# A first graph product in seven quarter products, with its column factors prepared a layer sooner

## The chip, the cores and the metric

One core of a Trainium2 chip runs the whole program. The metric is the device time of one execution in microseconds (us). Before the change it is 2473.33 us, the median of three runs (2473.07 to 2473.34).

## What is computed

Sixteen graphs (batches) with 1024 nodes, 128 features a node, and a 1024 x 1024 matrix adj each, all in float32. Two blocks follow each other. The first is one graph layer, the second four graph layers, and each block ends in a residual sum and a layer norm:

```python
# first block
degree = adj.sum(-1)[:, :, None]
s  = einsum('bid,bij->bjd', x, adj) / degree
x1 = layernorm(x + relu(concat([x, s]) @ W.T + b))
# second block: layers i = 0..3
src_agg = einsum('bjv,bij->biv', f @ ws + bs, adj / l2norm_of_rows)
dst_agg = einsum('bjv,bji->biv', f @ wd + bd, adj / l2norm_of_columns)
f = tanh(concat([src_agg, f @ wn + bn, dst_agg]) @ wu + bu)
# f of layers 2 and 3 is joined with inputs of earlier layers
out = layernorm(x1 + f)
```

A batch so needs adj itself, its transpose, the norms of its rows and columns, and one more sum per row (the degree).

## The kernel before

A batch is a sequence on TensorE of: messages and aggregation of layers 0, 1 and 2 of batch b, the first block of batch n = b + 1 (`first_gnn`), and messages and aggregation of layer 3 of batch b. The work that prepares batch n (its matrix, its sums, its factors, its transpose, its norm) is put between the matmuls of batch b. Four engines have a hand-written order: TensorE (PE), VectorE (DVE), ScalarE (ACT) and GpSimd (POOL) execute what the Python code issues, in that order; only SyncE (SP), which issues the DMAs, is ordered by the framework's scheduler. Where one instruction uses what another engine produced, a semaphore wait is added, and what is queued behind it on its engine waits too.

`aggregate` (L565) computes one layer as products of quarters: adj and the messages are cut into halves both ways, and seven products of sums of quarters take the place of eight (the scheme known as Strassen-Winograd). A product is four matmuls of a 128 x 64 stationary operand against 512 columns. Two such matmuls, one for the upper and one for the lower 64 rows of the output, go to TensorE as a pair; one pair is a step. Layers 0 and 1 have 30 steps, layer 2 has 32, layer 3 has 34: first two or more for the nodes' own features, then the products M1 to M4, Z11, Z12 and Z21, each with a DST half (adj, sums T) and a SRC half (adj transposed, sums Q). `events` read finished sums at fixed steps, and `hooks` is a table of step numbers at which other work is issued: a hook at 11 is issued ahead of step 11, on whatever engine its instructions belong to. `between` does the same for the four groups of `messages` (L504), which produce the tiles t and, on VectorE, their sums S1 to S4 (L529 to L532).

The parts that matter here:

- `first_gnn` (L424): x times adj in whole, 8 row blocks x 2 halves of columns = 16 pairs, each half scaled by dinv (the inverse of degree times norm), then four pairs with the weights.
- `sums` (L237): of a row block of the next matrix, the degree (on ScalarE for blocks 0 to 3, L249, on VectorE for 4 to 7, L251), the squares (ScalarE, L252), and their running sum acc on GpSimd (L254, L256). The tile sq has two places, so a square waits for the add that used its place before. For b over 0, blocks 0 to 7 are issued at steps 1, 2, 4, 6, 12, 15, 18 and 20 of layer 1.
- `column_sums` (L259) transposes and reduces acc on VectorE, in the messages of layer 2 (`between` 1); `inverses` (L288, a small matmul pc, then VectorE, then a power on GpSimd) at step 4 of layer 2; `inverse_rows` and `factor_row` (L319, L331) send the factors to DRAM and back, spread over all partitions as cinv; at step 10 `row_inverses` (L304), at step 18 the small matmul rp (`gather_inverses`, L312); at steps 12, 15, 19 and 25 `scale_columns` (L338) multiplies the next matrix by cinv, four row blocks by one half of columns at a time.
- The second norm of batch b - 1 runs in layer 1: y and its sum s (VectorE, L349, L354, L356) at step 0, the small matmul pm at step 11 (`norm_centre`, L359), pv and a power at step 17 (`norm_rstd`, L375); its end and its store are issued in layer 2 at step 4.
- `load(n)` (L190), the next matrix, is issued at step 5 of layer 0. It goes where the matrix of batch b - 1 was; that place serves in layer 3 as a staging place for the rows of adj that are to be transposed, the last of them rows[0], which is transposed at step 0 of the following layer 0 (`rows3`).

Of the kernel before, what the change touches and what calls it, by code (L numbers as in the profile page):

```python
# [8 lines left out]
F32 = mybir.dt.float32  # L9
AF = mybir.ActivationFunctionType  # L10
# [4 lines left out]
P = 128  # L15
# [8 lines left out]
def adj_resnorm_kernel(ctx: ExitStack, tc: tile.TileContext, x, adj, w0, b0, layers, out):  # L24
# [54 lines left out]
    def half(h):  # L79
        return slice(h * HW, (h + 1) * HW)  # L80
# [99 lines left out]
    def by_halves(out, x, y, start=True, stop=True):  # L180

        for s in (slice(V, P), slice(V)):
            nc.tensor.matmul(out[s], x[:, s], y, start=start, stop=stop)  # L183

    def product(name, i=None):
        if i is None:
            return ps_t.tile([P, HW], F32, tag="pt", name=name)
        return ps_p.tile([P, HW], F32, tag=f"p{i}", name=name)
# [47 lines left out]

    def sums(b, a, state, rows):  # L237

        if not state:
            state["cols"] = two.tile([P, 3 * NB], F32, tag="cols", name=f"cols{b}")  # L240
            state["acc"] = one.tile([P, N], F32, tag="row", name=f"acc{b}")
            state["inv"] = two.tile([P, C], F32, tag="inv", name=f"inv{b}")
            nc.gpsimd.memset(state["inv"][:, 3 * NB:], 0.0)
        cols, acc = state["cols"], state["acc"]
        for i in rows:
            sq = two.tile([P, N], F32, tag="sq", name=f"sq{b}_{i}")
            degree = cols[:, 2 * NB + i:2 * NB + i + 1]
            if i < BPH:
                nc.scalar.activation(sq, a[:, i, :], AF.Copy, accum_out=degree)  # L249
            else:  # L250
                nc.vector.reduce_sum(degree, a[:, i, :], axis=AX.X)  # L251
            nc.scalar.activation(sq, a[:, i, :], AF.Square, accum_out=cols[:, i:i + 1])  # L252
            if i == 1:
                nc.gpsimd.tensor_add(acc, state["sq"], sq)  # L254
            elif i > 1:
                nc.gpsimd.tensor_add(acc, acc, sq)  # L256
            state["sq"] = sq

# [164 lines left out]

    def first_gnn(b, xn, xT, a, dinv):  # L424

        agT = one.tile([P, N], F32, tag="acc", name=f"agT{b}")
        yT = one.tile([P, N], F32, tag="x", name=f"yT{b}")
        for h in (1, 0):
            s = half(h)
            pa = product(f"pa0_{b}_{h}")  # L430
            for i in range(NB):
                by_halves(pa, xn[:, i], a[:, i, s], i == 0, i == NB - 1)
            nc.vector.tensor_mul(agT[:, s], pa, dinv[:, s])
            if h == 1:
                combine_1(quarters(a))
        for h in (1, 0):
            first_weights(b, h, xT, agT, yT)
        return yT

    def first_weights(b, h, xT, agT, yT):  # L440
        s = half(h)
        pw = product(f"pw0_{b}_{h}")
        by_halves(pw, w0T[:, 0], xT[:, s], True, False)
        by_halves(pw, w0T[:, 1], agT[:, s], False, True)
        nc.scalar.activation(yT[:, s], pw, AF.Relu, bias=b0c)

# [33 lines left out]
    def quarters(a):  # L480
        return {(j, h): a[:, j * NJ:(j + 1) * NJ, half(h)] for j in range(2) for h in range(NH)}
# [8 lines left out]
    def combine_1(y):  # L490

        nc.vector.tensor_sub(y[0, 1], y[0, 1], y[0, 0])
# [72 lines left out]
    def aggregate(b, l, feats, msgs, a, at, T, Q, fT, etag, hooks={}, pieces=1):  # L565
# [81 lines left out]
        else:  # L647
# [3 lines left out]
            if l < NL - 1:  # L651
# [5 lines left out]
                (A, True, prod("M3", SRC)),  # L657
                (Z0, False, prod("Z21", SRC) + prod("Z21", DST)),
            ]
# [12 lines left out]

        def steps(groups, rows):
            flat = []
            for m, (acc, first, mms) in enumerate(groups):
                later = [g[1] for g in groups[m + 1:] if g[0] is acc]
                last = not later or later[0]
                for i, (x, y) in enumerate(mms):
                    flat.append((acc[rows], x, y, first and i == 0, last and i == len(mms) - 1))
            return flat  # L680

        up, lo = steps(upper, high), steps(lower, low)
        assert len(up) == len(lo)
# [230 lines left out]
    for b in range(B):  # L914
# [8 lines left out]
        if b == 0:  # L923
            def first_half0():
                nonlocal rinv
                to_x1(0)
                rinv = gather_inverses(0, row_inverses(0, inv))
                column_sums(0, st0)
                for q in (2, 3):
                    scale_rows(rows[q], q, rinv)  # L930

            t = messages(b, 0, feats, wm, {0: first_half0}, with_sums=False)
            cinv = {}
# [35 lines left out]
            def folded(l, part):  # L969
                return lambda *_: part(l, fetched[l])  # L970

            hooks = {2: lambda *_: inverses(0, st0, NB), 3: rows0, 5: folded(2, fold_begin), 7: cinv0,
                     8: folded(2, fold_end), 9: lambda *_: fold_and_scale(3, 0), 11: second0, 12: folded(3, fold_end),
# [5 lines left out]
            xs2 = load_spread(n)  # L979
        else:  # L980
            t = messages(b, 0, feats, wm)
            wm = message_weights(b, 1)
            w = {}
            Q = combined(b, "Q")
# [4 lines left out]

            def next_rows(w=w):  # L990
                combine_1(yt)
                if nxt:
                    w["a"] = load(n)

            hooks = {0: rows3, 3: lambda: combine(4, y, T), 5: next_rows, 7: lambda: combine(2, yt, Q),
                     9: lambda: combine(3, yt, Q), 11: lambda: combine(4, yt, Q)}
            aggregate(b, 0, feats, t, a, at, T, Q, f1, "row", hooks)
# [7 lines left out]

        def sums_of(i):
            return lambda: sums(n, a2, st, (i,))

        hooks = {}
        if b == 0:  # L1010
            def quarters2():
                for i in (2, 3, 4):
                    combine(i, yt, Q)

            hooks = {0: quarters2, 12: lambda: combine(4, y, T)}
            hooks |= {5 + 2 * i if i < 3 else 4 + 3 * i: sums_of(i) for i in ALL}
        else:
            nm = f"1_{b - 1}"
            w = {"ys": summed(f"y{nm}", "xa")}
            sums_of_next = dict(zip((1, 2, 4, 6, 12, 15, 18, 20), map(sums_of, ALL))) if nxt else {}  # L1020

            def begin1(w=w, nm=nm):
                norm_spread(w["ys"], f4, KS)
                w["s"] = norm_sum(w["ys"], KS, nm, back)

            def centre1(w=w, nm=nm):
                w["sq"] = norm_centre(w["ys"], w["s"], KS, nm)
                if nxt:
                    w["xs"] = load_spread(n)

            def squares1(w=w, nm=nm):
                w["v"] = norm_squares(w["sq"], KS, nm)

            def rstd1(w=w, nm=nm):
                w["r"] = norm_rstd(w["v"], KS, nm)

            hooks = {0: begin1, 11: centre1, 14: squares1, 17: rstd1, **sums_of_next}
        aggregate(b, 1, feats, t, a, at, T, Q, f23, "acc", hooks)
        second_norm = w if b else None
        if b:  # L1040
            xs2 = w.get("xs")

# [3 lines left out]

        def end1(w=second_norm):
            if b:
                norm_end(w["ys"], w["r"], KS)
                store(b - 1, w["ys"], KS)  # L1050

        def inverses3():
            inverses(n, st)
            end1()

# [19 lines left out]

        hooks, between = {4: end1}, {}
        if nxt:
            between = {1: sums3}
            hooks = {4: inverses3, 5: factors, 10: factors_of_rows, 11: start3, 12: lambda: scale(0, 1),
                     15: lambda: scale(NJ, 1), 18: factors_gathered, 19: lambda: scale(0, 0), 25: lambda: scale(NJ, 0)}  # L1080
        t = messages(b, 2, feats, wm, between)
        wm = message_weights(b, 3)
        aggregate(b, 2, feats, t, a, at, T, Q, f23, "acc", hooks)
        if nxt:
            dinv = factor_row(n, st, 2, "dinv")
            yT = first_gnn(n, w["xn"], w["xT"], a2, dinv)
            rinv = w["rinv"]
# [5 lines left out]
        if nxt:  # L1093
# [23 lines left out]

            def rstd0(w=w):
                w["r"] = norm_rstd(w["v"], KS, nm)


# [15 lines left out]

            def quarters0(w=w):
                w["T"] = combined(n, "T")
                for i in (2, 3):  # L1140
                    combine(i, y2, w["T"])
                scale_rows(rows[2], 2, rinv)

            def rows1(w=w):
                at2[1] = transposed(n, 1)
                transpose_rows(rows[2], 2, at2)
                scale_rows(rows[3], 3, rinv)
                w["back"] = take_back(b, kept)
                rows[0] = load_rows(n, 0, [place(0)])

# [23 lines left out]
        if nxt:  # L1174
            wm = message_weights(n, 0)
        aggregate(b, 3, feats, t, a, at, T, Q, f4, "row", hooks, 1 if nxt else 2)
        if nxt:
# [57 lines left out]
```

## Time and profile before

| | |
|---|---|
| median of three runs | 2473.33 us (2473.07 to 2473.34) |
| the profiled execution | 2473.83 us |
| its span (first to last instruction) | 2472.0 us |
| granted TensorE clock, mean | 0.998 |
| matmul time of one first product (16 pairs) | 13.73 us |
| GpSimd's add of 128x1024, mean (L256) | 2446 ns |
| SyncE: the next matrix, 8 DMAs of 512 KB | 12.2 us each to landing (median) |

The profile is of one execution. In its rows a start is in us from the span's start, then come the time taken, the engine, the line of the program, the operation, output<-input with shapes, and in brackets the idle time before it with the engine that ended it; "x2" rows merge neighbours. Rows of the chain have start, time, engine, output and line. PE is TensorE, DVE VectorE, ACT ScalarE, POOL GpSimd. A matmul of float32 shows as two records, so a pair is four.

### The profile page before, as it was taken

What the parts mean: (1) busy time and instruction counts of PE and PEld (TensorE: products, weight loads), DVE (VectorE), ACT (ScalarE), POOL (GpSimd) and SP (SyncE); (2) the same over time, 40 slices, a digit from 0 to 9 for tenths busy, and PEclk for the clock granted to TensorE, in tenths of its full rate; (3) what the DMA queues carried; (4) which work ended last, traced back from release to release, by engine and by line L of the source; (5) the groups of instructions that cost most, each with busy time, mean ns of one, the idle gap of its engine ahead of it and who ended that gap; (6) DMA issues with size and microseconds to landing.
All of it is one profiled execution on the core that took longest, in us unless ns stands there. A gap on an engine that the chain in (4) does not pass through costs nothing.

```text
span 2472.0 us, 30281 instructions
## 1 busy us (share of the span) xinstructions
PE 2457.1 (99%) x11573; PEld 1037.2 (42%) x11573; DVE 1689.8 (68%) x2075; ACT 843.1 (34%) x1569; POOL 524.8 (21%) x205
## 2 busy tenths in 40 slices
PE   8999999999999999999999999999999999999998
PEld 5443344433444344443434444334443344433444
DVE  5858667586775857668577685776858667586743
ACT  5415234152341513425143341433415234152321
POOL 4401304013040220402104030040311304013000
PEclk9999999999999999999999999999999999999999
DMA  9517245261543516335172442724427244261410
GB/s 206 101 48 150 51 96 104 63 135 43 115 92 74 117 43 135 77 85 101 46 150 59 98 88 60 152 44 102 94 58 143 52 97 103 64 134 44 94 24 9
DMA packets 363793, 219.66 MB, mean 89 GB/s; under 512 B 150848, under 2 KB 334912, under 8 KB 363648
## 3 DMA queue, kind: packets, MB, share of 16 engines
q1 hardware_dynamic: 362880, 215.36, 41.3%
q0 software_dynamic: 768, 2.36, 0.4%
q8 instruction: 92, 1.51, 0.3%
q14 instruction: 53, 0.43, 0.1%
HBM read 199.17 MB, written 18.46 MB: 88 GB/s over the span
## 4 chain that ended last, share of the span: by engine, by line
PE 97%; DMA 1%; SPq 1%; DVE 0%; ACT 0%; issue 0%; POOLq 0%; DVEq 0%
PE m L692 44%; PE z L692 26%; PE pt L514 16%; PE pa L183 8%; PE pw L183 2%; DMA raw<-in_L_gnn_ws_dram 1%; SPq L458 0%; PE z L562 0%; PE pm L183 0%; DMA a<-in_adj_dram 0%; PE d L562 0%; DMA raw<-in_L_gnn_bs_dram 0%; DMA rows<-in_adj_dram 0%; DMA raw<-in_L_gnn_wn_dram 0%; SPq L131 0%
## 5 line engine op out<-in xcount | busy, mean ns | idle before, releaser
L692 PE MATMUL m<-Q,S 128*64 128x512 f32 x1008 | 446.4, 593 | 0.0
L692 PE MATMUL m<-T,S 128*64 128x512 f32 x1008 | 396.4, 593 | 0.0
L692 PE MATMUL m<-at,t 128*64 128x512 f32 x1008 | 393.5, 593 | 0.0
L692 PE MATMUL m<-a,t 128*64 128x512 f32 x1008 | 390.6, 593 | 0.0
L382 POOL TENSOR_TENSOR rs<-ve,mhalf 128x32 f32<-128x32 f32 x30 | 169.4, 5645 | 871.5 <-DVE ve L380 871.5
L517 DVE TENSOR_TENSOR t<-pt,wm 128x512 f32<-128x512 f32 x256 | 175.4, 690 | 188.6 <-PE pt L514 188.0
L692 PEld LDWEIGHTS m<-Q,S 128*64 128x64 f32 x1008 | 135.7, 137 | 270.8 <-issue 260.9
L256 POOL TENSOR_TENSOR acc<-acc,sq 128x1024 f32<-128x1024 f32 x90 | 220.1, 2446 | 82.2 <-ACT sq L252 79.8
L692 PE MATMUL z<-at,S 128*64 128x512 f32 x504 | 230.1, 594 | 0.0
L692 PE MATMUL z<-T,t 128*64 128x512 f32 x504 | 226.8, 592 | 0.0
L692 PE MATMUL z<-a,t 128*64 128x512 f32 x504 | 226.8, 592 | 0.0
L692 PE MATMUL z<-at,t 128*64 128x512 f32 x504 | 226.6, 592 | 0.0
L692 PE MATMUL z<-a,S 128*64 128x512 f32 x504 | 226.6, 592 | 0.0
L692 PE MATMUL z<-Q,t 128*64 128x512 f32 x504 | 226.6, 592 | 0.0
L596 ACT COPY e<-m 64x512 f32<-64x512 f32 x63 | 36.7, 582 | 528.0 <-PE m L692 527.7
L514 PE MATMUL pt<-wm,f1T 128*128 128x256 f32 x768 | 213.6, 383 | 0.1
L183 PE MATMUL pa<-a,xn 128*64 128x512 f32 x960 | 208.5, 592 | 0.0
L340 DVE TENSOR_TENSOR a<-a,cinv 128x512 f32<-128x512 f32 x250 | 156.7, 694 | 75.5 <-DMA cinv<-dr 73.0
L254 POOL TENSOR_TENSOR acc<-sq,sq 128x1024 f32<-128x1024 f32 x15 | 41.6, 2770 | 761.7 <-ACT sq L252 761.7
L692 PEld LDWEIGHTS m<-at,t 128*64 128x64 f32 x1008 | 120.2, 137 | 143.9 <-issue 143.9
L692 PEld LDWEIGHTS m<-T,S 128*64 128x64 f32 x1008 | 118.9, 137 | 135.4 <-issue 135.4
L692 PEld LDWEIGHTS m<-a,t 128*64 128x64 f32 x1008 | 119.0, 137 | 126.1 <-issue 117.3
(196 smaller groups left out, 3960.9 us busy)
## 6 DMA issues: line engine op xcount, KB each, us to landing
a<-in_adj_dram SPq DMA_DIRECT2D x120, 512.0 KB, 12.2
a<-in_adj_dram SPq DMA_DIRECT2D x360, 128.0 KB, 3.9
rows<-in_adj_dram SPq DMA_DIRECT2D x240, 64.0 KB, 2.9
wm<-wsave SPq DMA_DIRECT2D x16, 512.0 KB, 3.9
xn<-in_x_dram SPq DMA_DIRECT2D x124, 64.0 KB, 2.1
wm<-wsave SPq DMA_DIRECT2D x31, 256.0 KB, 2.7
xs<-in_x_dram SPq DMA_DIRECT2D x60, 128.0 KB, 3.6
cinv<-dr SPq DMA_DIRECT2D x30, 256.0 KB, 5.2
```

Of the source, the lines that this page charges most:

```text
L183: nc.tensor.matmul(out[s], x[:, s], y, start=start, stop=stop)
L254: nc.gpsimd.tensor_add(acc, state["sq"], sq)
L256: nc.gpsimd.tensor_add(acc, acc, sq)
L340: engine.tensor_mul(a[:, i, s], a[:, i, s], cinv[:, s])
L382: nc.gpsimd.tensor_tensor(rstd, ve, mhalf[:, :n], ALU.pow)
L514: nc.tensor.matmul(pt[:, q], f[:, i * P:(i + 1) * P], wm[:, 1 + c], start=(k == 0), stop=(k == nch - 1))
L517: nc.vector.tensor_add(t[j][:, o:o + 2].rearrange("p k a v c -> p k (a v c)"), pt, wm[:, 0][:, None, :].to_broadcast([P, 2, 2 * P]))
L596: nc.scalar.copy(e0[high], A[high])
L692: nc.tensor.matmul(o, x, y, start=start, stop=stop)
```

## The change

For the batches 1 to 15, the first block's product x times adj is computed by the same scheme as the layers: seven products of four matmuls, 14 pairs in place of 16. It needs sums of quarters of x (`first_sums`, in a place of the tag sq) and of adj: T2 in the places of S2, S3, S4 and x, T3 in those of t0 and t1, T4 in that of the layers' T4. As T4 is overwritten, it is computed a second time in layer 3 (`rstd0`). In layers 1 and 2 the product Z21 has its DST half, which reads T4, ahead of its SRC half.

What prepares the next matrix is moved, for b over 0: its load to the beginning of layer 0; the degrees all to ScalarE, four of them at steps 17 and 19 of layer 0 and four in layer 1, as copies in place; the squares of blocks 0 and 1 both at step 1 of layer 1 and the others at 3, 5, 8, 12, 15 and 18; the column sums to step 23 and `inverses` to step 29 of layer 1; `inverse_rows` and `factor_row` to the first group of messages of layer 2; the four scalings to steps 4, 6, 8 and 10 of layer 2, `row_inverses` to 12, `gather_inverses` to 17, x's transpose to 20, and the new sums to 13, 16, 25 and 29. The end of the second norm moves to step 14 of layer 2, its pv behind layer 1. rows[0] gets places of its own (tags xa and acc). For b = 0 the old step numbers stay and the new sums are at 26, 27, 29 and 31. In batch 0 the row factors move behind the third group of messages.

```diff
-            pa = product(f"pa0_{b}_{h}")
-            for i in range(NB):
-                by_halves(pa, xn[:, i], a[:, i, s], i == 0, i == NB - 1)
-            nc.vector.tensor_mul(agT[:, s], pa, dinv[:, s])
-            if h == 1:
-                combine_1(quarters(a))
+        T3 = first_quarter_3(b, y, T2)
+        upper = [(A, True, prod(X[0, 0], y[0, 0])), (Bk, True, prod(S[2], T2)), (A, True, prod(S[3], T3, (0, 1))),
+                 (Z0, True, prod(X[1, 1], T4))]
+        lower = [(Ck, True, prod(S[1], y[0, 1])), (Z1, True, prod(S[4], y[1, 1])), (Dk, True, prod(S[3], T3, (2, 3))),
+                 (Z0, True, prod(X[0, 1], y[1, 0]))]
+        events = {4: m1_and_m4_read, 8: m2_read, 10: m3_read}
...
+    def first_quarter_2(b, y):
+        T2 = [one.tile([P, HW], F32, tag=tag, name=f"f2_{b}_{tag}") for tag in ("S2", "S3", "S4", "x")]
+        for k in range(NJ):
+            nc.vector.tensor_sub(T2[k], y[1, 1][:, k], y[0, 1][:, k])
+        return T2
...
+    def squares_of_row(b, a, state, i):
+        sq = two.tile([P, N], F32, tag="sq", name=f"sq{b}_{i}")
+        nc.scalar.activation(sq, a[:, i, :], AF.Square, accum_out=state["cols"][:, i:i + 1])
+        if i == 1:
             state["acc"] = one.tile([P, N], F32, tag="row", name=f"acc{b}")
+            nc.gpsimd.tensor_add(state["acc"], state["sq"], sq)
+        elif i > 1:
+            nc.gpsimd.tensor_add(state["acc"], state["acc"], sq)
+        state["sq"] = sq
...
-                (Z0, False, prod("Z21", SRC) + prod("Z21", DST)),
+                *((Z0, False, prod("Z21", part)) for part in ((SRC, DST) if l == NL - 1 else (DST, SRC))),
...
-            t = messages(b, 0, feats, wm, {0: first_half0}, with_sums=False)
+            t = messages(b, 0, feats, wm, {0: lambda: to_x1(0), 2: row_factors0}, with_sums=False)
...
+            if nxt:
+                w["a"] = load(n)
+                st = begin_sums(n)
             t = messages(b, 0, feats, wm)
...
+                     9: lambda: combine(3, yt, Q), 11: lambda: combine(4, yt, Q),
+                     17: lambda: degrees(0), 19: lambda: degrees(2)}
...
-            sums_of_next = dict(zip((1, 2, 4, 6, 12, 15, 18, 20), map(sums_of, ALL))) if nxt else {}
+            if nxt:
+                sums_of_next = {1: sums_of(0, 1), 3: sums_of(2), 5: sums_of(3, of=(4,)), 8: sums_of(4, of=(5,)),
+                                12: sums_of(5, of=(6,)), 15: sums_of(6, of=(7,)), 18: sums_of(7),
+                                23: lambda: column_sums(n, st), 29: lambda: inverses(n, st)}
...
-            hooks = {0: begin1, 11: centre1, 14: squares1, 17: rstd1, **sums_of_next}
+            hooks = {0: begin1, 11: centre1, 14: squares1, **sums_of_next}
         aggregate(b, 1, feats, t, a, at, T, Q, f23, "acc", hooks)
         if b:
-            xs2 = w.get("xs")
+            rstd1()
+            second_norm, xs2 = w, w.get("xs")
...
+            scales = [lambda: scale(0, 1), lambda: scale(NJ, 1), lambda: scale(0, 0), lambda: scale(NJ, 0)]
+            if b == 0:
+                between = {1: sums3}
+                hooks = {4: inverses3, 5: factors, 10: factors_of_rows, 11: start3, 18: factors_gathered,
+                         **dict(zip((12, 15, 19, 25), scales))}
+                quarters_at = (26, 27, 29, 31)
+            else:
+                between = {0: factors}
+                hooks = {**dict(zip((4, 6, 8, 10), scales)), 12: factors_of_rows, 14: end1, 17: factors_gathered, 20: start3}
+                quarters_at = (13, 16, 25, 29)
+            hooks |= dict(zip(quarters_at, (quarter1, x_sums, quarter2, quarter4)))
...
-            def rstd0(w=w):
+            def rstd0(w=w, y=y, T=T):
                 w["r"] = norm_rstd(w["v"], KS, nm)
+                combine(4, y, T)
...
+                rows[0] = load_rows(n, 0, [one.tile([P, QB // 2, NH * P], F32, tag=tag, name=f"rows0_{n}_{tag}")
+                                           for tag in ("xa", "acc")])
```

## The prediction

> **What bounds the kernel now.** I read the page first (busy shares, chain, groups), then the chain in order of time for one whole batch (b = 5, from 812.08 us), then the timelines of VectorE, GpSimd and ScalarE in its layer two (l = 1).
>
> ```profile
> PE 2457.1 (99%) x11573; PEld 1037.2 (42%) x11573; DVE 1689.8 (68%) x2075; ACT 843.1 (34%) x1569; POOL 524.8 (21%) x205
> ...
> PE 97%; DMA 1%; SPq 1%; DVE 0%; ACT 0%; issue 0%; POOLq 0%; DVEq 0%
> ...
> L183 PE MATMUL pa<-a,xn 128*64 128x512 f32 x960 | 208.5, 592 | 0.0
> ```
>
> TensorE is the bound, and nothing makes it wait. The third row is the product that the change shortens. The chain gives its price and the places of three small matmuls (start, duration):
>
> ```profile
> 754.79 13.73 PE pa L183 x64
> ...
> 847.15 7.72 PE m L692 x36
> 854.88 0.18 PE pm L183 x4
> ...
> 871.52 7.10 PE pt L514 x32
> 878.62 3.58 PE z L692 x16
> 882.20 0.09 PE pc L183 x4
> ```
>
> Sixteen pairs of 64-column matmuls take 13.73 us, 0.858 a pair; a layer advances by one such step at a time. The batches repeat every 151.68 us (754.79 to 906.47). pm, pc and the like read a VectorE result in the middle of TensorE's queue: late results stop TensorE there. VectorE around pm:
>
> ```profile
> 846.05 0.76 DVE L529 TENSOR_TENSOR S<-t 128x256 f32<-128x256 f32 x2
> 846.85 0.69 DVE L530 TENSOR_TENSOR t<-t,t 128x512 f32<-128x512 f32 x1
> 847.57 0.69 DVE L531 TENSOR_TENSOR S<-t 128x512 f32<-128x512 f32 x1
> 848.30 2.73 DVE L532 TENSOR_TENSOR S<-t,S 128x512 f32<-128x512 f32 x1
> 850.95 1.23 DVE L349 STREAM_TRANSPOSE y<-f23T 128x1024 f32<-128x1024 f32 x1
> 852.22 1.23 DVE L354 TENSOR_TENSOR y<-y,xk 128x1024 f32<-128x1024 f32 x1
> 853.48 1.22 DVE L356 TENSOR_REDUCE s<-y 128x32 f32<-128x1024 f32 x1
> ```
>
> GpSimd at that time, then ScalarE, which feeds it:
>
> ```profile
> 847.71 2.77 POOL L254 TENSOR_TENSOR acc<-sq,sq 128x1024 f32<-128x1024 f32 x1 [53.03 <-ACT sq L252]
> 852.99 5.13 POOL L256 TENSOR_TENSOR acc<-acc,sq 128x1024 f32<-128x1024 f32 x2 [2.51 <-ACT sq L252]
> ```
> ```profile
> 843.04 1.04 ACT L249 ACTIVATE sq<-a 128x1024 f32<-128x1024 f32 x1
> 844.20 1.06 ACT L252 ACTIVATE sq<-a 128x1024 f32<-128x1024 f32 x1
> ```
>
> Two things count. The sum s ends at 854.70 and pm starts at 854.88: no slack. And L532, 0.69 us elsewhere, took 2.73: it began 0.6 us into GpSimd's add, and ended 0.55 after it (850.48).
>
> [...] The trace agrees: 2.73 against 0.69 above, and L621 2.32 at 863.58 inside the add of 862.99 to 865.35; it also shows the turns: GpSimd asked during L531 and went before L532. The reduces (L251, L356) ran at 1.21 beside adds[...]
>
> **The change, part by part.** Measured against the profiled execution: 2473.83 us (span 2472.0 and 1.8 around it), 0.5 over the median.
>
> *Matmuls.* Seven products of four matmuls are 28, 14 pairs for 16: 2 x 0.858 = 1.72 a batch, 15 batches, 25.7 us. The four weight pairs stay. On the path in full: TensorE is the path.
>
> *First product's own operations.* T2, T3 and T4 are 12 subtractions of 128x512 at 0.614 (the rate of L340: 8 in 4.91), 7.4 us; the sums of x are four of half that, some 1.6; eight at 0.69 end it; the two agT multiplies (0.69 each) go. For b over 0, counting on from pc (below): x's transpose must wait until y1 has been stored out of the same place (5.4 us from L387's end to L345 in the trace), after that T2 is complete 1.7 us before TensorE's step 4 of the product asks for it, T3 meets step 8 within 0.1, e1 and e0 are 1.3 and 0.7 ahead of the weight pairs. TensorE's own 14 pairs are the cover: cost 0, at most 0.5 a batch. The T4 recomputed in layer four (2.29) fits into VectorE's 5.54 us wait on GpSimd before L387: 0; uncovered it would be 2.29. DST before SRC in Z21 only frees T4 four steps sooner: 0.
>
> *b = 0.* Its scalings stay at steps 12 to 25 and end at 151.74 in the trace; then combine_1 2.28, two x sums 0.8: 154.9, where TensorE wants them at 148.07: 6.9 us of wait; T3 then misses step 8 by 1.4. Cost 8.4 once (bounds 6 and 9).
>
> *Load of the next matrix, rows0, SP.* The load moves from 824.17 to the end of the transposes at 812.08. In the order of the built program its first DMA stands ahead of eight rows0 DMAs, and the other seven behind them. Rows0: 8 x 0.47 to 0.64 from 812.6, landing 2.9 later: 819.3 to 820.7, scaled by four ScalarE steps of 0.42 by 822.4; the transpose comes up at about 822.5. 0, at most 0.5. The load's first half is in about 15 us after 812 (eight DMAs took some 18 before), ahead of degrees at 829.
>
> *Degrees.* Four ScalarE copies of 1.06 go between m1's and m4's copies of layer one, a gap of 5.67 us: 0. The other four leave VectorE (1.21 each) for ScalarE in layer two. The in-place copy changes nothing.
>
> *Squares, layer two.* Without degrees 0 and 1, the second square ends 2.32 sooner, so GpSimd's first add asks at 845.39 instead of 847.71, and runs to 847.75 (2.36). That is ahead of S3 (L529) at 846.05, which now waits to 847.6; S1 ends at 849.10. Square 2 starts as the first add ends, and the second add asks at 849.07 (1.29 after it); S2 asks at 849.14. 0.07 decides, less than I trust these rows with. (a) Add first: S2 ends 851.98, add three (queued) 854.20, S4 854.75, transpose 855.98, L354 behind add four 858.06, s 859.32, pm 859.50 for 854.88: TensorE 4.6 late. (b) S2 first: add two ends 852.04, S4 852.6, transpose 853.8, L354 behind add three 855.9, s 857.16, pm 857.34: 2.5 late. Lowest, if VectorE wins each further turn: s 855.2, 0.5. S3's own wait (1 us at step 2) is inside these. Queued behind pm is the whole of TensorE.
>
> *Column sums before the end of layer two (steps 23 and 29).* From s: centre 1.6, its square 1.1, degree and square 2.2, m4 copies 1.3, degree and square 2.2, add six 2.6, VectorE's e0 add behind it 0.5, add seven 2.2, e1 add behind that 0.6, transpose and reduce 2.5, handing over 0.3: 17.1 to pc. TensorE needs 0.18 + 18 x 0.858 after pm, and pm is 0.18 after s: 15.8. Wait 1.3, in (a) and (b) alike.
>
> *Scaling sooner.* Before, pc 882.20 to the first scaling 896.54 took 14.34 (sums, power on GpSimd 3.8, two DMAs). Now all 16 multiplies come next: 9.82, then row_inverses 0.15: 24.4 with the hand-over. TensorE gets from pc (step 29) to the rp matmul (step 17 of layer three) in 0.09 + 0.86 + 0.09 + 7.10 + 3.58 + 13 x 0.86 = 22.9. rp waits 1.5; behind it is all of TensorE. Bounds 0.8 to 2, as the DMAs land. Before, rp stood at step 18 with only tiny work ahead of it. The statistics' pv and power at the end of layer two hide behind the messages: 0.
>
> *Start.* rp and pc of batch 0 move later; TensorE waited 1.9 for sp once: gain about 1.
>
> **Sum.** 2473.8 - 25.7 + 8.4 - 1.0 = 2455.5. For the 14 batches b = 1 to 14: (a) 4.6 + 1.3 + 1.5 = 7.4, making 2559; (b) 5.3, making 2530. I take the middle, 6.4, since the turn may fall either way, batch by batch: 2455.5 + 89.6 = 2545. Lowest: 0.5 + 1.3 + 1.5 = 3.3, 2502.
>
> **Rivals.**
> - *The adds don't hold VectorE up this time.* Then s and the column sums are ready in time and only rp waits, 1.5: 2455.5 + 21 = 2476.5, no change. For: S3 has never overlapped an add in the trace. Against: every other two-input operation that did was held.
> - *Faster: all hidden.* Place: the scalings of layer three. If they begin 1.5 us sooner after pc, by a quicker power (2.91 at 126.81) and DMAs, and the adds cost nothing, rp is ready and 2455.5 is left. It decides from 14.34 down to 12.8. Against: VectorE waited for cinv in all 15 batches.
> - *More:* as (a), and rows0 or T3 late by 0.5 each: 2573.
> - That fewer matmuls are not issued is excluded: the built order has 14 pairs.
>
> **Numbers.** 0.2% (about 5 us) is what a measurement tells from no change. Main case with its bounds 2502 to 2562: 0.80, all slower; more than that 0.05; no change 0.07, of which 0.02 over the 5 us; faster 0.08. So slower 0.87, same 0.05, faster 0.08. The range 2495 to 2575 takes in the main case, the worse one and some us of rounding below, and leaves out the other two rivals and tails, about 0.18.
>
> **What would show it.** Period of the first product 154 to 159 us instead of 149.96; VectorE's S3 at over 2 us in layer two, one or two more of S2, S4, L354 stretched; TensorE idle before pm, pc and rp, named as waiting for s, part and sp; 7 us before batch 1's product. If S3 takes 0.4, or TensorE stays at 99%, the main case is wrong; if pm is on time while pc waits, the turns are.

## The result, and the profile after

The changed kernel takes 2548.99 us, the median of four runs (2547.21 to 2552.26), against 2473.23 before (with a fourth run of it): a ratio of 1.0308, 95% interval 1.029 to 1.0326. Its profiled execution took 2547.21 us (span 2545.4), 73.4 more than that of before.

TensorE issues fewer matmuls and is still the busiest engine, but the chain no longer lies on it alone. The page of after, shares of the span and then the chain by engine:

```profile
PE 2469.9 (97%) x11453; PEld 1041.9 (41%) x11453; DVE 1912.2 (75%) x2394; ACT 952.4 (37%) x1786; POOL 540.3 (21%) x205
...
PE 17%; DVE 4%; DMA 2%; issue 1%; SPq 0%; POOL 0%; ACT 0%; DVEq 0%; POOLq 0%; ACTq 0%
```

Before, 11573 matmul records and PE with 97% of the chain; now 120 fewer (15 products by two pairs of four records), and VectorE and DMAs on the chain. (The chain that the page follows back covers a quarter of the span here, so I read from it only which engines appear.) What TensorE waits for is in its own view of waits (us in total, times, longest):

```profile
PE pm L183 <- DVE s L358: 44.9, 14, 3.2
PE m_f L512 <- DVE xn L440: 5.9, 1, 5.9
...
PE m_f L512 <- ACT e_f L489: 2.9, 3, 1.4
PE m L770 <- DVE Q L583: 2.2, 5, 0.8
PE rp L183 <- DVE sp L309: 2.1, 2, 1.2
PE pc L183 <- DVE part L272: 1.8, 3, 0.6
```

pm stops TensorE in each of the 14 batches whose layer two prepares a next matrix, for 3.2 us; batch 1's sums of x once, for 5.9; the other waits are short and rare, rp and pc among them. (Layers one, two and three are from here on, as in the prediction, what the sections ahead of it call layers 0, 1 and 2.) Where pm's delay comes from shows in VectorE's timeline in layer two, the counterpart of the rows of before (S3 is now L616, S1 L617, S2 L618, S4 L619):

```profile
2122.52 2.26 DVE L616 TENSOR_TENSOR S<-t 128x256 f32<-128x256 f32 x2
2124.82 0.69 DVE L617 TENSOR_TENSOR t<-t,t 128x512 f32<-128x512 f32 x1
2125.54 2.79 DVE L618 TENSOR_TENSOR S<-t 128x512 f32<-128x512 f32 x1
2128.36 2.73 DVE L619 TENSOR_TENSOR S<-t,S 128x512 f32<-128x512 f32 x1
2131.02 1.23 DVE L351 STREAM_TRANSPOSE y<-f23T 128x1024 f32<-128x1024 f32 x1
2132.29 2.11 DVE L356 TENSOR_TENSOR y<-y,xk 128x1024 f32<-128x1024 f32 x1
2134.43 1.22 DVE L358 TENSOR_REDUCE s<-y 128x32 f32<-128x1024 f32 x1
```

and in GpSimd's:

```profile
2121.81 2.35 POOL L256 TENSOR_TENSOR acc<-sq,sq 128x1024 f32<-128x1024 f32 x1 [49.67 <-ACT sq L253]
2125.42 7.89 POOL L258 TENSOR_TENSOR acc<-acc,sq 128x1024 f32<-128x1024 f32 x3 [1.26 <-ACT sq L253]
```

Before, S3, S2 and the addition of xk took 0.76, 0.69 and 1.23 and S4 alone was held (2.73). Now S3 (2.26), S2 (2.79), S4 (2.73) and the addition (2.11) are: each waited for the addition on GpSimd that began before it. Taken one by one, the three additions of the last row took 2.36, 2.69 and 2.69: an addition that came up behind another waited in its turn for the operation of VectorE that the other one held. S1 ran free (0.69), in the 1.26 us in which GpSimd waited for the third square. In the kernel before, too, the operations held inside an addition read both operands from SBUF (L532 2.73 for 0.69, L621 2.32 for 0.69). L517, which reads pt from PSUM, took its 0.69 in all 30 cases that begin inside an addition, as at 873.48, with the additions of 871.18 to 875.96. An operation of the first kind is what the prediction calls a two-input one.

Where the time went, by stretches of TensorE's own sequence. Each number is a mean over these 14 batches, worked out from starts in the trace: from the first matmul of the first product to the weights (batches 2 to 14), layer one's products with the messages that follow them, layer two from its first own-feature matmul to pm, from pm to the messages of layer three, and layer three from its first matmul to the next first product:

| us | first product | layer one | to pm | pm to messages | layer three | batch 1's product |
|---|---|---|---|---|---|---|
| before | 13.73 | 29.55 | 9.54 | 16.69 | 27.75 | 13.73 |
| after | 12.33 | 29.80 | 14.02 | 18.27 | 27.78 | 20.36 |

A first product without a wait is 12.02. The sum: 15 x 1.71 less; batch 1's wait 8.3; 13 x 0.31; 14 x 0.25; 14 x 4.48; 14 x 1.58; 14 x 0.03; and 2.0 less at the start. That is -25.7 + 8.3 + 4.0 + 3.5 + 62.7 + 22.1 + 0.4 - 2.0 = 73.3, against 73.4 measured. So 85 of the us lie in layer two.

The 22.1 behind pm look like the late pc that I had forecast, and are mostly not. Columns: window in us, then busy time (and instructions) of PE, PEld, DVE, ACT and POOL, the granted TensorE clock, DMA share and GB/s. The first three windows lie around pm in one batch, the last two in another:

```profile
2132.12:2135.53 3.41, 0.38 (x1) 0.00 (x0) 3.34 (x3) 0.52 (x1) 1.20 (x1) 1.00 0.02 3
2135.53:2138.94 3.41, 3.23 (x12) 1.22 (x14) 1.69 (x3) 1.44 (x2) 0.00 (x0) 0.50 1.08 151
2138.94:2142.36 3.42, 3.42 (x18) 1.12 (x16) 0.87 (x1) 3.38 (x7) 1.64 (x1) 1.00 0.00 0
879.43:882.84 3.41, 1.60 (x6) 0.27 (x2) 3.38 (x3) 1.70 (x3) 2.41 (x1) 1.00 0.00 0
882.84:886.25 3.41, 2.02 (x14) 0.88 (x16) 2.52 (x3) 0.35 (x1) 0.00 (x0) 1.00 0.76 115
```

and TensorE's rows in the first of the two batches:

```profile
2135.71 0.43 PE L183 MATMUL pm<-s,fold 128*64 128x32 f32 x4 [3.20 <-DVE s L358]
...
2136.83 1.06 PE L770 MATMUL m<-T,S 128*64 128x512 f32 x1
...
2137.68 1.06 PE L770 MATMUL m<-T,S 128*64 128x512 f32 x1
...
2139.60 0.59 PE L770 MATMUL m<-T,S 128*64 128x512 f32 x1
```

For 3.41 us TensorE ran at a granted clock of 0.50: matmuls start 0.85 apart in place of 0.43, which costs half of that time, 1.7. In 11 of the 14 batches the trace has such a run of long matmuls behind pm, and there the stretch is 18.3 to 18.5; in the other three (17.6) there is none, and it is there that pc waits for its sum, 0.6.

The falls of the clock behind pm last 3.413 us each, one in batch 1's product (from 148.98) twice that, and they start whole multiples of 3.413 us apart. Cut into windows on this grid from batch 1's product on, the trace has a fall behind every window in which TensorE was recorded idle for 1.99 us or more (3.03 in the first row above), and behind none with 1.95 or less. All 14 waits for pm last 3.2; in the three batches without a fall a border of the grid splits the idle time into 1.81 and 1.39 (the last two rows above), 1.95 and 1.26, 1.67 and 1.54. So in this trace where a wait falls on the grid decides, beside its length.

### The profile page after: what moved, and what is told of

The parts are those of the page before. It is cut to its first block, busy times and chain, and to the rows that moved or that the text cites. A ratio compares the mean times of both kernels' runs of the same rounds, so it can differ in the third digit from the quotient of the medians.

```text
span 2545.4 us, 30905 instructions
## 1 busy us (share of the span) xinstructions
PE 2469.9 (97%) x11453; PEld 1041.9 (41%) x11453; DVE 1912.2 (75%) x2394; ACT 952.4 (37%) x1786; POOL 540.3 (21%) x205
## 3 DMA queue, kind: packets, MB, share of 16 engines
q0 software_dynamic: 768, 2.36, 0.4%
## 5 line engine op out<-in xcount | busy, mean ns | idle before, releaser
L770 PE MATMUL m<-T,S 128*64 128x512 f32 x1008 | 413.8, 612 | 1.6
L770 PE MATMUL m<-at,t 128*64 128x512 f32 x1008 | 413.5, 612 | 0.0
L384 POOL TENSOR_TENSOR rs<-ve,mhalf 128x32 f32<-128x32 f32 x30 | 192.5, 6415 | 973.5 <-DVE ve L382 973.5
L258 POOL TENSOR_TENSOR acc<-acc,sq 128x1024 f32<-128x1024 f32 x90 | 230.5, 2561 | 145.7 <-ACT sq L253 141.7
L256 POOL TENSOR_TENSOR acc<-sq,sq 128x1024 f32<-128x1024 f32 x15 | 35.7, 2379 | 704.4 <-ACT sq L253 704.4
L770 PE MATMUL z<-T,t 128*64 128x512 f32 x384 | 172.9, 592 | 0.0
L601 PEld LDWEIGHTS pt<-wm,f1T 128*128 128x128 f32 x768 | 143.3, 190 | 32.8 <-ACT f1T L783 12.8
```

What stands on the lines that cost most here:

```text
L256: nc.gpsimd.tensor_add(state["acc"], state["sq"], sq)
L258: nc.gpsimd.tensor_add(state["acc"], state["acc"], sq)
L384: nc.gpsimd.tensor_tensor(rstd, ve, mhalf[:, :n], ALU.pow)
L601: nc.tensor.matmul(pt[:, q], f[:, i * P:(i + 1) * P], wm[:, 1 + c], start=(k == 0), stop=(k == nch - 1))
L770: nc.tensor.matmul(o, x, y, start=start, stop=stop)
```

## The experiments

All twelve are timed against the kernel before in the same set of runs; ratios are to it.

**1. Less work in the kernel before.** What remains of the change is only that the first addition moves.

```diff
+            if b > 1:
+                nc.gpsimd.memset(state["cols"][:, 2 * NB:2 * NB + 2], 1.0)
-            if i < BPH:
+            if b > 1 and i < 2:
+                pass
+            elif i < BPH:
```

> The kernel before with two operations of ScalarE left out in 14 batches: the row sums (degrees) of blocks 0 and 1 at the start of layer two, 1.04 us each; their columns are set to 1 instead, so the row factors of those blocks are not the reference's. Everything else stays as it was, on TensorE too. Main theory (GpSimd's first addition, moved 2.2 us sooner, holds VectorE's S3 and the turns after it): less work, yet S3 takes over 2 us and the matmul pm comes 2.5 to 4.6 us late in each of 14 batches: 35 to 64 us more than before, 2508 to 2537. Rival (the loss came from the new product or from TensorE, not from where the addition falls): no change, 2473, or a little less.

2487.72 us, ratio 1.0063 (1.0048 to 1.0078). Two operations fewer a batch cost 15 to 16 us (15.0 between the profiled spans): the direction is the theory's and excludes the rival, since nothing of the new product is in this kernel. The size is not: 1.1 a batch, 0.4 up to pm and 0.7 behind it. GpSimd, then VectorE (S3 is L533, S2 L535, S4 L536):

```profile
849.50 2.35 POOL L258 TENSOR_TENSOR acc<-sq,sq 128x1024 f32<-128x1024 f32 x1 [50.63 <-ACT sq L256]
854.37 5.82 POOL L260 TENSOR_TENSOR acc<-acc,sq 128x1024 f32<-128x1024 f32 x2 [2.51 <-ACT sq L256]
```
```profile
850.21 2.26 DVE L533 TENSOR_TENSOR S<-t 128x256 f32<-128x256 f32 x2
852.51 0.69 DVE L534 TENSOR_TENSOR t<-t,t 128x512 f32<-128x512 f32 x1
853.24 0.69 DVE L535 TENSOR_TENSOR S<-t 128x512 f32<-128x512 f32 x1
853.96 0.69 DVE L536 TENSOR_TENSOR S<-t,S 128x512 f32<-128x512 f32 x1
```

Only S3 is held. GpSimd pauses 2.51 us between the first two additions, not 1.26 as in the changed kernel, since here ScalarE still makes degree 2 in between; S2 and S4 fit into the pause. The first addition alone makes pm 0.4 late, and the other 4.1 of the 4.5 must come from the ones behind it.

**2. One addition in place of seven.**

```diff
-        if i == 1:
+        if i == (1 if b == 1 else 7):
             state["acc"] = one.tile([P, N], F32, tag="row", name=f"acc{b}")
...
-        elif i > 1:
+        elif i > 1 and b == 1:
```

> The changed kernel with six of GpSimd's seven additions left out in 14 batches (the last two squares alone are added, so the column sums are not the reference's). Main theory: no addition is left in the first half of layer two, so VectorE's S operations take 0.7 us again and pm is on time (4.5 us a batch back), and the column sums end sooner, so pc is on time too (1.5 back): 2549 minus 14 times 6.0 is 2465. Rival (the waits come from VectorE's own longer list, or from ScalarE's order of squares): pm or pc stay late, 2500 to 2549.

2463.42 us, ratio 0.9965 (0.9952 to 0.9978): as expected. The stretch to pm is 9.49, that behind it 16.73 with pc's own matmuls in it; no half-rate run is left behind pm (mean clock 0.998). The whole 6 us a batch in layer two hang on the additions; 0.3 in layer one and 0.3 in the first product stay.

**3. Degrees 0 and 1 back ahead of their squares.**

```diff
-            hooks = {..., 17: lambda: degrees(0), 19: lambda: degrees(2)}
+            hooks = {..., 17: lambda: degrees(2)}
-                sums_of_next = {1: sums_of(0, 1), ...}
+                sums_of_next = {1: both, ...}
+            def both():
+                sums_of(0, of=(0,))()
+                sums_of(1, of=(1,))()
```

> The changed kernel with the degrees of blocks 0 and 1 put back directly ahead of their squares in layer two, as before (those of blocks 2 and 3 stay in layer one). Nothing is left out. It adds no work, and gives ScalarE 2.2 us more before the second square. Main theory: the first addition falls behind S1 again and holds S4 alone; pm is on time (0 to 0.5 late instead of 4.5), pc stays 1 to 3 late: 14 times 3 to 4.5 less, 2486 to 2507. Rival (that additions overlap S operations at all, wherever they start, is what costs): pm 2 or more late still, over 2515.

2500.28 us, ratio 1.0115 (1.0098 to 1.0132), inside the theory's range. S3 and S2 are free again, yet pm is 1.8 late, more than its 0 to 0.5, close to the rival's 2: the first of three additions in a row now holds the addition of xk (VectorE, then GpSimd):

```profile
862.60 2.98 DVE L356 TENSOR_TENSOR y<-y,xk 128x1024 f32<-128x1024 f32 x1
```
```profile
862.12 8.12 POOL L258 TENSOR_TENSOR acc<-acc,sq 128x1024 f32<-128x1024 f32 x3 [1.26 <-ACT sq L253]
```

TensorE's wait for pm is 1.6 here, and no half-rate run follows in any batch (mean clock 0.998); pc waits 0.6 in all 14.

**4. Batch 1's product in whole pairs.**

```diff
+            if b:
-            hooks |= dict(zip(quarters_at, (quarter1, x_sums, quarter2, quarter4)))
+                hooks |= dict(zip(quarters_at, (quarter1, x_sums, quarter2, quarter4)))
+        if b == 0:
+            dinv = factor_row(n, st, 2, "dinv")
+            yT = first_gnn_whole(n, w["xn"], w["xT"], a2, dinv)
...
```

> The changed kernel with batch 1's first product in 16 pairs on the scaled matrix, as before, instead of quarter products (its scalings end too late for them). Nothing is left out. Main theory: the 8.4 us that this one product waits for the quarter sums go, its own 1.7 come back: 6.6 us less, 2542 to 2543. Rival (the wait comes from the scalings themselves and stays): 2549 or more.

2539.90 us, ratio 1.0276 (1.026 to 1.0291), 2 below the expected. The product takes 13.73 in place of 20.36, which is the 6.6; the rest is within the spread of the runs (2537.19 to 2543.95).

**5. A pause between the additions, first try.**

```diff
-                 17: lambda: degrees(0), 19: lambda: degrees(2)}
+                 17: lambda: degrees(0), 19: lambda: degree3()}
-                sums_of_next = {1: sums_of(0, 1), 3: sums_of(2), ...}
+                sums_of_next = {1: sums_of(0, 1), 3: sums_of(2, of=(2,)), ...}
```

> The changed kernel with one degree of ScalarE, that of block 2, put back ahead of its square in layer two (degrees 0, 1 and 3 stay in layer one); nothing is left out. GpSimd's first addition still comes before S3, but the second asks 1.04 us later, when S2 and S4 are already under way, as it did in the run that left degrees 0 and 1 out. Theory as it stands after that run (the first addition costs 1 us through S3; the other 3.5 come from the second and third additions taking their turns ahead of S2, S4 and the addition of xk): the layer waits 1 to 1.5 us in place of 4.5, so 14 times 3 to 3.5 less: 2500 to 2507. Rival (the first addition decides, the later ones only follow it): over 2535.

2549.91 us, ratio 1.0309 (1.0295 to 1.0323), as the rival has it. But ScalarE's timeline shows that the edit moved nothing:

```profile
867.21 1.04 ACT L248 ACTIVATE a<-a 128x1024 f32<-128x1024 f32 x1
868.15 0.19 ACT L248 ACTIVATION_READ_ACCUMULATOR a<-a 128x1 f32 x1
869.83 1.06 ACT L253 ACTIVATE sq<-a 128x1024 f32<-128x1024 f32 x1 [1.49 <-POOL acc L256]
```

The square waits for its tile until the first addition (867.43 to 869.79) has read it; the degree, a copy in place, needs no tile and ran during the wait. The kernel before writes the degree's copy into the square's tile, so that it starts only after the addition. This run decides nothing; run 9 repeats it with that one difference.

**6. The store sooner.**

```diff
-                hooks = {..., 12: factors_of_rows, 14: end1, ...}
+                hooks = {..., 12: lambda: (factors_of_rows(), end1()), ...}
```

> The changed kernel with the last multiply of y1 and its four store DMAs in layer three issued right after the operation for rp, ahead of the first quarter's subtraction (2.28 us sooner) instead of behind it. Nothing is left out. Theory: x's transpose, which waits for the store (SyncE needed 3.1 us for the four DMAs in one batch and 5.1 in another), is no longer late, so the first product takes 12.0 us in every batch instead of 12.3 on average from batch 2 on: 14 times 0.3 is 4 less, 2543 to 2546. Rival (the late batches come from another wait): no change, 2549.

2546.59 us, ratio 1.0297 (1.0282 to 1.0311). That is just above the expected, and not by its reason: the first product is 12.28 on average against 12.33. In the changed kernel x's transpose waits for the store in every batch, 1.6 to 4.1 us, and the late products are those where it waits over 2.2. SyncE, then VectorE, in such a batch of the changed kernel:

```profile
922.73 0.91 SPq L336 DMA_DIRECT2D dinv<-dr  x2
926.17 5.12 SPq L235 DMA_DIRECT2D out_dram<-y  x4
```
```profile
934.10 1.25 DVE L347 STREAM_TRANSPOSE x_T<-xs 128x1024 f32<-128x1024 f32 x1 [4.05 <-DMA out_dram<-y]
```

The four stores follow two DMAs that spread dinv over all partitions, and 2.28 us sooner they are still behind them: SyncE then takes 4.8 to 6.5 us to give them out, where it took 3.0 to 5.1. Run 11 puts them in front.

**7. All of it together.** Runs 3, 4 and 6, with degree 2 back as well, two squares moved ahead of the centred one and three degrees on VectorE, whose reduces of 1.21 us took no longer beside an addition in the kernel before.

```diff
...
-                sums_of_next = {1: sums_of(0, 1), 3: sums_of(2), 5: sums_of(3, of=(4,)), 8: sums_of(4, of=(5,)),
-                                12: sums_of(5, of=(6,)), 15: sums_of(6, of=(7,)), 18: sums_of(7),
+                sums_of_next = {1: both, 3: sums_of(2, of=(2,)), 5: sums_of(3, of=(4,)), 10: sums_of(4, 5),
+                                12: sums_of(of=(5, 6), engine=nc.vector), 15: sums_of(6),
+                                17: sums_of(of=(7,), engine=nc.vector), 18: sums_of(7),
...
-                hooks = {..., 12: factors_of_rows, 14: end1, 17: factors_gathered, 20: start3}
+                hooks = {..., 11: end1, 12: factors_of_rows, 19: factors_gathered, 20: start3}
```

> All that the runs so far point to, nothing left out: quarter products from batch 2 on and 16 whole pairs for batch 1; degrees 0, 1 and 2 ahead of their squares in layer two as before, 3 in layer one, 4 on ScalarE, 5 to 7 on VectorE; squares 4 and 5 ahead of the square of the centred y; y1's last multiply and store ahead of the first quarter, the rp matmul two steps later. Theory (where the additions fall is the whole loss): pm 0 to 0.5 late, pc 0 to 1.0 late, first product and layer one 0 to 0.5: from 2457 with no wait, 14 times 0 to 1.5 more: 2457 to 2478, the middle below the kernel before. Rival (moving them only shifts the collision to the additions of layer two's end): pc 2 or more late, 2485 and over.

2480.82 us, ratio 1.003 (1.0019 to 1.0041): between the two ranges. pc is on time (16.78 behind pm), and pm 1.75 late as in run 3, for the same reason.

**8. pc behind layer three's first messages.**

```diff
-                                23: lambda: column_sums(n, st), 29: lambda: inverses(n, st)}
+                                23: lambda: column_sums(n, st)}
...
-                between = {0: factors}
+                between = {0: lambda: inverses(n, st), 1: rstd1, 2: factors}
```

> The combined version with the pc matmul and what follows it moved from step 29 of layer two to behind the first message matmuls of layer three, and the rstd and factor operations one and two groups later; nothing is left out. Theory: pc gets 2.6 us of slack and is never waited for; the scalings begin up to 2.7 us later, so that the first product's quarters may be late by up to 2: 2455 to 2485. Rival (pc wasn't late in the combined version): no better than it, slower by the quarters.

2530.46 us, ratio 1.0228 (1.0214 to 1.0242): worse than either theory. The wait moved to rp, 26.7 us in 15 cases, and layer three takes 29.94 for 27.63 in run 7. From pc to the scalings and rp there is no 2.7 us to give away.

**9. The pause, second try.** As run 5, with degree 2 written into the square's tile.

```diff
         sq = two.tile([P, N], F32, tag="sq", name=f"sq{b}_{i}")
+        if i in of:
+            nc.scalar.activation(sq, a[:, i, :], AF.Copy, accum_out=state["cols"][:, 2 * NB + i:2 * NB + i + 1])
...
-                sums_of_next = {1: sums_of(0, 1), 3: sums_of(2), ...}
+                sums_of_next = {1: sums_of(0, 1), 3: lambda: squares_of_row(n, a2, st, 2, (2,)), ...}
```

> The changed kernel with the degree of block 2 put back ahead of its square in layer two, now written into the square's own tile as before (it waits there until the first addition has freed the tile); in the run before, the in-place copy ran during that wait and moved nothing. Degrees 0, 1 and 3 stay in layer one; nothing is left out. So only now the second addition asks 1.04 us later, when S2 and S4 are under way. Theory (the first addition costs 1 us through S3, the other 3.5 come from the additions behind it going ahead of S2, S4 and the addition of xk): pm's stretch of the layer is 0.4 to 1.0 too long in place of 4.5, the rest of the layer 1 to 2.5: 14 times 3 to 4 less, 2493 to 2507. Rival (the first addition decides, the later ones only follow): over 2535.

2492.60 us, ratio 1.0083 (1.0068 to 1.0099): the theory holds and the rival is out. One operation of 1.04 us a batch that has to wait for a tile, where in run 5 it did not, takes 57 us off (2549.91 to 2492.60). GpSimd, then VectorE (S3 is L618, S2 L620, S4 L621):

```profile
852.58 2.36 POOL L258 TENSOR_TENSOR acc<-sq,sq 128x1024 f32<-128x1024 f32 x1 [48.77 <-ACT sq L255]
857.45 8.28 POOL L260 TENSOR_TENSOR acc<-acc,sq 128x1024 f32<-128x1024 f32 x3 [2.51 <-ACT sq L255]
```
```profile
853.29 2.27 DVE L618 TENSOR_TENSOR S<-t 128x256 f32<-128x256 f32 x2
...
856.32 0.69 DVE L620 TENSOR_TENSOR S<-t 128x512 f32<-128x512 f32 x1
857.04 0.69 DVE L621 TENSOR_TENSOR S<-t,S 128x512 f32<-128x512 f32 x1
```

The stretch to pm is 9.91 (4.1 less), and no half-rate run follows in any batch (mean clock 0.998). Behind pm it is 18.27 all the same, for other reasons: 0.7 as in run 1, where the two rows of matmuls fall out of step at S3 and meet again behind pm, and pc, which now waits 0.6 in all 14 batches; some 0.2 more I can't place.

**10. The same in the combined version.** Degrees 0, 1 and 2 written into the squares' tiles.

```diff
-                sums_of(0, of=(0,))()
-                sums_of(1, of=(1,))()
+                for i in (0, 1):
+                    squares_of_row(n, a2, st, i, (i,))
...
-                sums_of_next = {1: both, 3: sums_of(2, of=(2,)), ...}
+                sums_of_next = {1: both, 3: lambda: squares_of_row(n, a2, st, 2, (2,)), ...}
```

> The combined version with the degrees of blocks 0, 1 and 2 written into the squares' tiles, as before, so that the second addition again asks after VectorE's addition of xk has begun; nothing is left out. Theory: the 1.8 us that the combined version still waits for pm go (the addition of xk takes 1.2 us again instead of 3.0), pc stays on time or comes up to 0.5 late: 25 less than the combined version's 2481, or 18 at least: 2454 to 2463, below the kernel before. Rival (the later addition then holds the sums at the layer's end, and pc takes the wait over): 2470 and over.

2496.93 us, ratio 1.0098 (1.0084 to 1.0112): the rival. pm is on time (9.54), and pc takes the wait over: 26.2 us in 14 cases, longest 1.9. In six of them TensorE's clock falls behind that wait (0.57 over 4 us in one), and layer three's messages, which come there, take 8.1 to 8.8 in place of 7.1.

**11. The stores ahead of the scalings.**

```diff
-                hooks = {..., 11: end1, ...}
+                hooks = {..., 3: end1, ...}
```

> The same with y1's last multiply and its four stores ahead of the scalings, where VectorE waits for the column factors, instead of behind them; nothing is left out. Theory: the place that x's transpose needs is free 11 us sooner, so no first product comes late (0.4 a batch on average in the combined version), and the multiply is hidden: 14 times 0.3 to 0.4, 4 to 6 less than the run with the degrees in the squares' tiles: 2448 to 2459. Rival (the multiply, 1.2 us, pushes the scalings and rp): the same or up to 10 more.

2490.05 us, ratio 1.0073 (1.006 to 1.0086). The level is wrong by run 10's miss. The median is 7 below run 10's, the profiled executions differ by 1.5 only, so the size of the gain stays open; what is plain is that every first product of the batches 2 to 14 takes 12.02. SyncE gives the four stores out in 2.7 us, away from dinv.

**12. The first addition ahead of S3, on purpose.**

```diff
-                 17: lambda: degree3()}
+                 17: lambda: degrees(0), 19: lambda: degree3()}
-                sums_of_next = {1: both, ...}
+                sums_of_next = {1: sums_of(0, 1), ...}
```

> The version with the stores first, with the degrees of blocks 0 and 1 moved back into layer one, where the change has them (that of block 2 stays written into its square's tile); nothing is left out. So the first addition starts ahead of S3 and the second only once S2 and S4 are done, as in the run with degree 2 after the first addition, and squares 4 and 5 come ahead of the centred square. Theory: the first addition costs the 1.06 us through S3 that two runs show, and for it all seven additions end soon enough for pc, so that neither pm nor pc stops TensorE further: layer two 1.0 to 1.3 over its 26.3, layer one 0.3 over, first product 12.0: a period of 151.2 to 151.7 and 2461 to 2469, 3 to 11 below the kernel before. Rival (pc still late, by 1 or more, since GpSimd's seven additions and VectorE's turns between them are longer than the layer): 2478 or more, and no version of this kind beats the kernel before.

2469.05 us, ratio 0.9986 (0.9979 to 0.9992), at the upper end of the expected: 3.2 below the kernel before, and the fastest of all that compute the whole. To pm it takes 9.91, behind pm 17.78, so layer two is 1.5 over, for 1.7 that each product saves, and layer one is 0.2 over. Batch for batch next to nothing is gained: from the first product of batch 1 to that of batch 15 it is 2122.9 us for 2123.5, and the rest of the profiled gain of 4.9 is 2.5 before the first of them and 1.7 in the last.

## Why the prediction was right

The forecast was 2545 and the result 2548.99. The main mechanism held, additions on GpSimd that hold VectorE up; that the sum came so close is in part luck, as some terms were wrong and cancel.

- **Matmuls, -25.7:** 13.73 to 12.02, 1.71 a product. Right.
- **Batch 1, +8.4** (its parts, 6.9 and 1.4, make 8.3)**:** 20.36 for 12.02, 8.3. Run 4 shows the cause, quarter sums that come late, but the parts were others: the wait was 5.9, no wait for T3 followed, and behind the wait TensorE ran at a clock of 0.50 for 3.0 us (152.83 to 155.80), which costs 1.5. What is left, 0.9, I can't place.
- **Start, -1.0:** the first product of batch 1 begins 2.0 sooner (145.89 for 147.90). The wait for sp is 1.0 shorter (0.88 for 1.87), as forecast; before, a half-rate run of 3.41 us followed it (from 40.96), and now none does, which is probably the rest.
- **pm, 4.6 in case (a), 2.5 in (b):** (a) came in all 14 batches, 4.48. The mechanism is shown by runs 1, 2 and 9: 0.4 up to pm with the first addition alone, 4.1 more with those that follow it without a pause. The middle was a hedge: the turns fell alike in every batch.
- **pc, 1.3:** the size was near (1.5) and the reason wrong in 11 batches of 14. There TensorE runs at half rate after pm, which costs 1.7 and makes pc's own lateness vanish. In the three without it pc waits 0.6. The step that failed is that TensorE's 15.8 us from pm to pc were taken at full rate. That the half rate comes of the wait, and not of the new work, rests on runs 2, 3 and 9: where the wait is gone or 1.6, no half-rate run follows pm, though the new product is there; and in runs 10 and 11 the half-rate runs moved with the wait, from pm to pc.
- **rp, 1.5:** next to nothing in 13 batches and 1.2 in one. The term that was mis-sized is the way from pc to the first scaling, 14.34, which I took from one batch of before; in the batch of the rows above it is 12.57 (2153.07 to 2165.64). Counted alike from pc's first matmul, the 14 batches before have 13.9 on average (14.5 in the one that I took), those after 12.9; rp waits where it is longest, 14.4. GpSimd, then VectorE after:

```profile
2153.94 2.91 POOL L304 TENSOR_TENSOR inv<-cols,mhalf 128x16 f32<-128x16 f32 x1 [4.74 <-DVE cols L303]
```
```profile
2165.64 9.72 DVE L342 TENSOR_TENSOR a<-a,cinv 128x512 f32<-128x512 f32 x16 [0.70 <-DMA cinv<-dr]
```

  and before, VectorE, then GpSimd:

```profile
883.12 1.22 DVE L387 TENSOR_TENSOR y<-y,rs 128x1024 f32<-128x1024 f32 x1
```
```profile
883.29 3.82 POOL L302 TENSOR_TENSOR inv<-cols,mhalf 128x16 f32<-128x16 f32 x1 [7.33 <-DVE cols L301]
```

  The power took 2.91 in place of 3.82, in every one of these batches, which is most of the difference of 1.0. Before, it came up 0.17 behind the last multiply of the second norm (L387), which has two inputs in SBUF: here it was GpSimd that waited, by all appearances, as the power took 2.91 at 126.81, where no such multiply is near. The change moves the multiply to step 14 of layer three. The turns that cost 4.5 at pm so gave 0.9 back, an estimate (3.82 less 2.91), as no run tried this by itself. 12.57 + 9.72 + 0.15 is 22.4, under TensorE's 22.9. This is the place of the "all hidden" rival: its condition, below 12.8, was met in 10 of the 14 batches, and it lost since its other one, additions that cost nothing, was not.
- **First product, 0 to 0.5, and rows0, 0 to 0.5:** 0.31 and 0.25 on average. Inside their bounds, though entered with 0 (single batches reach 1.65 and 0.98); they add 7.5 us. The first is the store behind dinv (runs 6 and 11). For the second, rows0's DMAs stand behind the next matrix's first DMA on SyncE, as foreseen; that this is the cause isn't shown, as no run tried another order.
- **The in-place copy changes nothing:** not so once a degree stands ahead of a square that waits for its tile. Runs 5 and 9 differ in that alone: the copy in place takes the pause away, and 57 us go with it.

By terms, 14 x (4.6 + 1.3 + 1.5) would have been 104 and 14 x 6.4 was 90; measured are 85 in layer two, 0.4 in layer three and 7.5 elsewhere. A middle between (a) and (b), 0.9 too low for pm, met an rp term 1.5 too high.

## What to carry to other kernels

In these runs VectorE paid for additions on GpSimd (S2 2.79 for 0.69), so ask of a freed engine which addition it will start sooner, and which operations of VectorE with both operands in SBUF then stand behind it; a pause between two additions that was 1.3 us longer (2.51 for 1.26) in 14 batches was worth 57 us here. In these runs a wait of TensorE of 1.9 to 3.2 us could cost another 1.7 behind it, and waits of 1.6 did not, so a wait need not be gone altogether before the larger part of its cost is. Before an operation is used as a spacer, look at what it waits for: one without a tile to wait for disappeared into the gap (run 5).

## What the runs showed of the hardware

- The granted clock fell to 0.50 behind some waits of TensorE and not behind others: after 1.6 us of waiting for pm in none of 42 batches (runs 3, 7 and 8), after 1.9 for pc in 13 of 28 (runs 10 and 11), after 3.2 for pm in 11 of 14 (the changed kernel). Length alone did not decide: in run 8 it fell behind a wait for rp of 1.99 and not behind one of 2.51, which a border of the grid splits into 1.48 and 1.03. With 1.8 to 2.0 us of idle time in one window of the grid it went either way in these runs: it fell behind 1.87 (37.55 to 40.96, the kernel before) and not behind 1.95 (1036.44 to 1039.86, the changed kernel). The mean clock of the whole run, 0.991 for 0.998, hardly shows it.
- In a row of additions, an operation of VectorE with both operands in SBUF got in after the addition that it met (2.79, 2.73 and 2.98 us for operations of 0.69, 0.69 and 1.23). The next addition in the row then took 2.69 or 3.22 in place of 2.36, so the two engines took turns. GpSimd's power took 3.82 where a multiply of VectorE had begun 0.17 before (14 batches of the kernel before), and 2.91 without it.
- Four stores of 128 KB took SyncE 2.6 to 2.9 us by themselves (run 11), and 3.0 to 6.6 right behind two DMAs that spread a row over all partitions (the changed kernel, runs 6 and 7).
